# A four-layer graph network on one NeuronCore: LSTM operand copies on another engine, and a new order of work at the end of two layers

## The chip, the cores and the metric

The kernel runs on one core of a Trainium2 chip. The core has five engines with a queue of instructions each: TensorE (PE: matmuls and transposes; PEld is its loading of the stationary operand), VectorE (DVE), ScalarE (ACT), GpSimd (POOL) and SyncE (SP, which here only issues DMAs). They wait for one another through semaphores. The metric is the device time of one execution in microseconds (us), the median of several runs.

## The reference, cut to what matters

`x` is 128 batches x 64 nodes x 256 features in float32, `adj` a 64 x 64 matrix. Four layers of the form `x = x + gnn(relu(layernorm(x)), adj)` follow one another:

```
# layer 0: two graph convolutions, then an LSTM over windows of nodes
h = relu(adj @ (x @ Wg0 + bg0)); h = relu(adj @ (h @ Wg1 + bg1))
for p in 1, 2, 3, 4:                  # a window is p neighbouring nodes
    wins = h[:, :nw * p].reshape(B * nw, p, H)
    last = lstm_last(Wih[p-1], Whh[p-1], bih[p-1], bhh[p-1], wins)
    h[:, arange(nw) * p + (p - 1)] = last
# layer 1: attention over 512 edges, 4 heads
Xq, Xv = H @ W_lin.T, H @ W_val.T
e = sum(leaky_relu(Xq[:, src] + Xq[:, dst]) * a) + log(A0[src, dst] + EPS)
attn = softmax of e over the edges with the same src
Y = segment_sum(attn * Xv[:, dst], src) @ W_out.T
# layer 2: A_hat @ h, then two linear maps with batch norms
# layer 3: dense graph attention with a masked softmax
```

The layer norm is over the 256 features of a token. Each LSTM window of p nodes takes p steps of `g = x_t @ Wih.T + h @ Whh.T + bias` with the gates i, f, g, o.

## The kernel before, in words

The 8192 tokens are worked in 16 chunks of 512 tokens (128 tokens on the partitions, four such tiles to a chunk); a group is four chunks. The kernel is written with a framework that puts the instructions of each engine into a queue by its own scheduler; an instruction wrapped in `late` (L71 to L73) keeps its place in the program's order. Every queue runs in order. Tiles come from pools with a fixed number of buffers, and a load into a buffer waits until the last reader of its earlier content is done.

**Layer 0, convolutions** (`graph_convolutions`, L492, driven by the loop from L549). A chunk passes through stages; one round of the loop takes each chunk under way one stage on, oldest first, and the tables of a later layer are built in between. The class `Norm` (L78) takes mean and variance on VectorE, then 1/sqrt either on POOL with four small instructions (L99 to L102) or, with `root_on_scalar`, on ScalarE and VectorE (L95 to L97), and then ScalarE writes the scaled `h` (L109). Chunk 0 alone uses `root_on_scalar`. `bdA` is a block-diagonal matrix with `adj` twice; its matmul with `h` stands at L50.

**Layer 0, LSTM** (class `Step`, L582). The nodes' states lie transposed, features on partitions, in `hT`. The work is ordered by half of the groups, and in each half by phases w = 1, 2, 3, 4 (the window's length), in each phase by pairs of parts (so many windows at once) and by step t. A 2 x 2 block product is made with seven products in place of eight, so each operand is needed as seven blocks: three copies and four differences. `prepare` (L604) makes the seven for `x_t`: for w > 1 POOL copies (L619, L620) from the strided `hT` into the tile `xop`, VectorE subtracts (L621, L627, L628). It is called at the second-to-last gate of the step before. `product` (L638) runs the matmuls of one gate into PSUM tiles `pa`, `pb`, `pc`; ScalarE copies and functions (L666, L681, L686, L688) and VectorE adds (L682, L691, L696) empty them. The last step of a window ends with VectorE writing `hT` (L731). The class `Weights` (L414) loads a phase's weights with a DMA on SP and makes their four sums on POOL (L430): `wih` and `sih` with two buffers, `whh` and `shh` with one. `phase_over` asks for the next ones at the end of a phase. When a group has gone through w = 4, `group_out` (L763) transposes it back on PE (L165), adds it to the residual on VectorE (L168), stores it with a DMA of POOL's queue to `xa` in DRAM (L770) and loads the group of the second half into its place with SP (L773). It stands right behind the group's last gate.

**Layer 1** (L864 to L1216). `project`, `gather` and `score` run per tile and pair of tiles. Each group's `edge_softmax` (L968) is a generator whose steps are taken one by one between other work (`behind`, `step_behind`): scans and reciprocals on VectorE, transposes on PE (L997), VectorE's `attn` (L1000), eight indirect DMAs of POOL that scatter it into a dense field in DRAM (L1026), and two DMAs that bring the field back (L1012), one for each half of the partitions. Then, per chunk, `values_of` runs `weigh` (matmuls L1073 of the turned attention `att` with the values `xv`) and, one chunk later, `put_out` (matmuls L1093 with `wout`, VectorE's add of the residual L1103, the statistics of the next norm on VectorE L1109 and L1110, four small POOL instructions L1112 to L1115). `fetch` (L1041) loads `xv` and `xo` (four buffers) on SP and turns the attention with two copies (L1055, one on ScalarE and one on VectorE), one chunk ahead. `flush_stores` (L1149) stores the result to `xb`. Layer 2 begins with `scale_x` (L1197), loads of `xb` (L1230) and the matmuls with `bdH` (L50).

The order around the change:

```
for one in list(under_way):                      # convolutions, oldest first
...
if k == len(step.gates) - 2 and at + 1 < len(steps):
    steps[at + 1].prepare()
...
if step.w == MAX_SKIP and step.t == MAX_SKIP - 1:
    for c in range(2):
        group_out(step.g, c)
...
for n in range(4, NCH):                          # layer 1, second part
    for _ in range(6):
        step_behind()
```

## Time and profile before

| what | us |
|---|---|
| runs, device time | 2151.81, 2152.57, 2156.58 |
| median | 2152.57 |
| the profiled execution's own time | 2154.34 |
| its span | 2152.6 |
| PE busy | 2049.1 |
| DVE, ACT, POOL busy | 1354.9, 1123.4, 425.9 |
| layer 0, convolutions (0 to 80): PE busy | 65.4 |
| layer 0, LSTM (80 to 1310): PE busy | 1195.5 |
| layer 1 (1310 to 1765): PE busy | 425.8 |
| layer 2 (1765 to 1990): PE busy | 216.4 |
| layer 3 (1990 to 2152.6): PE busy | 146.0 |

The last five rows are from the trace's windows, with borders put by eye where one layer's matmuls give way to the next one's; the layers overlap a little. A stage's length less its PE time is the time in which PE stands. The mean granted clock of PE over the span was 0.981 of full speed. In the profile's lines an arrow in brackets, [1.56 <-DVE hT L731], gives the idle time ahead of an instruction and what ended it: engine, what it wrote, and its line in the kernel.

### The profile page before, as it was taken

What the parts mean: (1) busy time and instruction counts of PE and PEld (TensorE: products, weight loads), DVE (VectorE), ACT (ScalarE), POOL (GpSimd) and SP (SyncE); (2) the same over time, 40 slices, a digit from 0 to 9 for tenths busy, and PEclk for the clock granted to TensorE, in tenths of its full rate; (3) what the DMA queues carried; (4) which work ended last, traced back from release to release, by engine and by line L of the source; (5) the groups of instructions that cost most, each with busy time, mean ns of one, the idle gap of its engine ahead of it and who ended that gap; (6) DMA issues with size and microseconds to landing.
All of it is one profiled execution on the core that took longest, in us unless ns stands there. A gap on an engine that the chain in (4) does not pass through costs nothing.

```text
span 2152.6 us, 25600 instructions
## 1 busy us (share of the span) xinstructions
PE 2049.1 (95%) x9444; PEld 1362.6 (63%) x9444; DVE 1354.9 (63%) x2425; ACT 1123.4 (52%) x2160; POOL 425.9 (20%) x576
## 2 busy tenths in 40 slices
PE   7999999999899999999999998999999789999898
PEld 5777478766688746886668884333334665534686
DVE  6665666554555567556546555576776757786675
ACT  3344766544454467555445444566565356591444
POOL 4110011310301022003002112113212420000662
PEclk9999999999999999999999999999999999999899
DMA  8321000100100340001000024113314761022012
GB/s 282 103 85 68 0 21 1 40 0 1 39 1 1 118 156 20 0 1 40 0 24 16 0 69 152 59 40 103 93 60 126 207 208 59 0 69 88 30 60 69
DMA packets 94028, 135.06 MB, mean 63 GB/s; under 512 B 6352, under 2 KB 82000, under 8 KB 91600
## 3 DMA queue, kind: packets, MB, share of 16 engines
q1 hardware_dynamic: 87600, 109.11, 15.4%
q0 software_dynamic: 5696, 24.12, 3.8%
q8 instruction: 74, 1.21, 0.2%
q14 instruction: 50, 0.41, 0.1%
q10 hardware_dynamic: 608, 0.20, 0.0%
HBM read 87.28 MB, written 46.14 MB: 62 GB/s over the span
## 4 chain that ended last, share of the span: by engine, by line
PE 84%; DVE 5%; POOL 3%; ACT 3%; DMA 2%; issue 1%; ACTq 0%; POOLq 0%; DVEq 0%
PE pa L638 26%; PE bank L50 21%; PE pc L638 12%; PE pair L50 6%; PE pb L638 6%; PE pa L1279 5%; PE pc L1279 2%; PE pb L1279 1%; POOL sih L430 1%; PE bank L1093 1%; PE bank L165 1%; ACT gate L666 1%; POOL shh L430 1%; PE pair L1532 1%; PE pair L1564 1%
## 5 line engine op out<-in xcount | busy, mean ns | idle before, releaser
L666 ACT ACTIVATE gate<-gate,bias 128x256 f32<-128x256 f32 (+2 forms) x368 | 248.4, 678 | 227.5 <-DVE gate L682 118.9
L638 PE MATMUL pa<-xop,sih 128*128 128x256 f32 (+2 forms) x1056 | 352.0, 423 | 5.8 <-ACT gate L681 3.4
L638 PEld LDWEIGHTS pa<-xop,sih 128*128 128x128 f32 x1056 | 202.2, 193 | 79.8 <-issue 23.6
L638 PE MATMUL pc<-xop,wih 128*128 128x256 f32 (+2 forms) x736 | 252.5, 425 | 0.0
L619 POOL COPY xop<-hT 128x512 f32<-128x512 f32 (+1 forms) x44 | 60.3, 1371 | 799.2 <-issue 411.3
L638 PE MATMUL pa<-lstm_h,shh 128*128 128x256 f32 (+1 forms) x672 | 212.7, 398 | 0.0
L951 DVE SCALAR_TENSOR_TENSOR lr<-lr 128x1024 f32<-128x1024 f32 x128 | 153.5, 1230 | 87.1 <-ACT lr L950 84.3
L682 DVE TENSOR_TENSOR gate<-pb,gate 128x256 f32<-128x256 f32 (+2 forms) x184 | 87.4, 475 | 160.0 <-PE pb L638 123.5
L638 PEld LDWEIGHTS pc<-xop,wih 128*128 128x128 f32 x736 | 141.4, 192 | 52.3 <-issue 23.9
L696 DVE TENSOR_TENSOR gate<-pc,gate 128x256 f32<-128x256 f32 (+2 forms) x184 | 87.4, 475 | 106.9 <-PE pc L638 105.8
L638 PEld LDWEIGHTS pa<-lstm_h,shh 128*128 128x128 f32 x672 | 127.7, 190 | 30.2
L950 ACT COPY lr<-pair 128x1024 f32<-128x1024 f32 x128 | 125.0, 1015 | 34.3 <-PE pair L50 34.3
L638 PE MATMUL pc<-lstm_h,whh 128*128 128x256 f32 (+1 forms) x448 | 141.8, 398 | 0.0
L681 ACT COPY gate<-pa 128x256 f32<-128x256 f32 (+2 forms) x184 | 76.9, 418 | 124.2 <-PE pa L638 123.7
L666 ACT ACTIVATE gate<-pa,bias 128x256 f32<-128x256 f32 (+2 forms) x184 | 94.5, 514 | 83.7 <-PE pa L638 83.5
L50 PE MATMUL pair<-sd_hot,xq 64*128 64x512 f32 x512 | 134.4, 622 | 0.3 <-ACT lr L950 0.3
L50 PE MATMUL bank<-wlv,hT 128*128 128x512 f32 x256 | 122.7, 611 | 7.0 <-ACT hT L154 7.0
L638 PE MATMUL pb<-xop,wih 128*128 128x256 f32 (+1 forms) x320 | 103.3, 407 | 8.9 <-POOL xop L619 8.9
L691 DVE TENSOR_TENSOR gate<-pa,gate 128x256 f32<-128x256 f32 (+2 forms) x184 | 87.4, 475 | 37.2 <-PE pa L638 34.4
L638 PE MATMUL pa<-xop,wih 128*128 128x256 f32 (+1 forms) x320 | 102.7, 403 | 6.6 <-POOL xop L619 5.0
L638 PEld LDWEIGHTS pc<-lstm_h,whh 128*128 128x128 f32 x448 | 85.1, 190 | 20.1
L50 PEld LDWEIGHTS bank<-wlv,hT 128*128 128x128 f32 x256 | 44.8, 189 | 81.9 <-issue 62.1
(319 smaller groups left out, 3857.6 us busy)
## 6 DMA issues: line engine op xcount, KB each, us to landing
field<-sd_hot SPq DMA_DIRECT2D x8, 1152.0 KB, 10.8
wih<-in_WihT SPq DMA_DIRECT2D x8, 1024.0 KB, 5.1
xres<-in_x SPq DMA_DIRECT2D x16, 512.0 KB, 5.6
xa<-xres POOLq DMA_DIRECT2D x16, 512.0 KB, 5.9
xo<-xa SPq DMA_DIRECT2D x16, 512.0 KB, 4.3
dense<-field POOLq DMA_DIRECT2D x8, 1024.0 KB, 11.4
xb<-xo SPq DMA_DIRECT2D x16, 512.0 KB, 5.2
xin<-xb SPq DMA_DIRECT2D x16, 512.0 KB, 4.1
```

Source lines behind the costliest of these rows:

```text
L50: nc.tensor.matmul(o, lhsT, rhs, start=start, stop=stop)
L430: nc.gpsimd.tensor_tensor(o, x, y, op)
L619: nc.gpsimd.tensor_copy(self.as_nodes(v[:, 0:2]), self.nodes(slice(0, 2), t))
L638: ins = nc.tensor.matmul(p[:, : self.N], weights[kind, self.phase](k, q), x[k], start=first_ and kind == "ih", stop=kind == "hh" or not se ...
L666: nc.scalar.activation(out, in_, AF.Tanh if q == 2 else AF.Sigmoid, bias=bias[:, self.w - 1, 2 * q + j : 2 * q + j + 1],)
L681: nc.scalar.copy(blk[0, 0], pa[:, :N])
L682: nc.vector.tensor_tensor(blk[0, 0], pb[:, :N], blk[0, 0], ALU.add)
L691: nc.vector.tensor_tensor(blk[1, 1], pa[:, :N], blk[1, 1], ALU.add)
L696: nc.vector.tensor_tensor(blk[1, 0], pc[:, :N], blk[1, 0], ALU.add)
L950: nc.scalar.copy(lr, p)
L951: nc.vector.scalar_tensor_tensor(lr, lr, 0.2, lr, ALU.mult, ALU.max)
L1279: ins = nc.tensor.matmul(p, lhs[k], x[k], start=first_, stop=last_one, skip_group_check=True)
```

## The change

- `add_transposed`: the first transpose is `late`; so is the making of `mask3` (a table of layer 3) on VectorE. The copies into `bdA` go from VectorE to POOL.
- All 16 chunks' norms in the convolutions take `root_on_scalar`, and a round of the loop begins with the newest chunk.
- `prepare`: the two copies go from POOL to ScalarE.
- `phase_over`: the ih weights of a later phase are asked for eight gates later.
- `prepare` for the first w = 1 step of the second half is called at the last gate of the step before.
- `group_out` runs one gate (first half of the chunks) and two gates (second half) after the group's last gate, and after the last gate at the end of the layer.
- Layer 1: four steps of the last softmax follow the last `edges`, seven more come at chunk 4; the first of its transposes is `late`. Its field comes back in four DMAs instead of two.
- `fetch` loads `xv` and x two chunks ahead, and the copies of the attention are a function of their own, `turn_attention`, two chunks ahead also, with exceptions around chunk 12. The x of the last three chunks lies in tiles of other pools.
- The statistics and the POOL instructions behind `put_out` are a function `sums`; at chunks 3, 4 and 5 they are held back to a later chunk.

No arithmetic on the data changes but for the root (square root and reciprocal in place of a power).

```diff
                 k = (i2 * 2 + c) * P
-                nc.tensor.transpose(
+                ins = nc.tensor.transpose(
                     p[:, k : k + P], src[:, c, col + i2 * P : col + (i2 + 1) * P], ident
                 )
+                if k == 0:
+                    late(ins)
         nc.vector.tensor_tensor(
...
-            nc.vector.tensor_scalar(mask3, adj2, 0.0, NEG, ALU.is_equal, ALU.mult)
+            late(nc.vector.tensor_scalar(mask3, adj2, 0.0, NEG, ALU.is_equal, ALU.mult))
             yield
...
                 r = slice(h * T, (h + 1) * T)
-                nc.vector.tensor_copy(bdA[r, r], adjT2[r, :])
+                nc.gpsimd.tensor_copy(bdA[r, r], adjT2[r, :])
...
-                h = Norm(coming.pop(n), n == 0).all()
+                h = Norm(coming.pop(n), True).all()
                 if 4 <= n + 3 < NCH:
...
                     under_way.append(graph_convolutions(n))
-                for one in list(under_way):
...
+                for one in under_way[-1:] + under_way[:-1] if n < NCH else list(under_way):
                     if next(one, 0) == 0:
...
                 v = x[:, : 7 * N].rearrange("p (q n) -> p q n", n=N)
-                nc.gpsimd.tensor_copy(self.as_nodes(v[:, 0:2]), self.nodes(slice(0, 2), t))
-                nc.gpsimd.tensor_copy(self.as_nodes(v[:, 2:3]), self.nodes(slice(3, 4), t))
+                nc.scalar.copy(self.as_nodes(v[:, 0:2]), self.nodes(slice(0, 2), t))
+                nc.scalar.copy(self.as_nodes(v[:, 2:3]), self.nodes(slice(3, 4), t))
                 nc.vector.tensor_tensor(
...
             if ph + 2 < len(phases):
-                weights["ih", ph + 2] = Weights("ih", phases[ph + 2])
+                later_weights.append((slot + 8, ph + 2))
             nxt = ph + 1 if ph + 1 < len(phases) and phases[ph + 1] > 1 else ph + 2
...
+        later_weights = []
         tasks = [(s, q, k) for s in range(len(steps)) for k, q in enumerate(steps[s].gates)]
         flight = []
-        later = []
+        later, outs = [], []
         norm_steps = iter(())
...
                 at, k = new[0], new[2]
-                if k == len(step.gates) - 2 and at + 1 < len(steps):
+                while outs and outs[0][0] <= slot:
+                    group_out(*outs.pop(0)[1:])
...
+                new_half = at + 1 < len(steps) and at and steps[at + 1].w == 1 < step.w
+                if k == len(step.gates) - (1 if new_half else 2) and at + 1 < len(steps):
                     steps[at + 1].prepare()
...
             next(norm_steps, None)
+            while later_weights and later_weights[0][0] <= slot:
+                _, ph = later_weights.pop(0)
+                weights["ih", ph] = Weights("ih", phases[ph])
             if old:
...
                     if step.w == MAX_SKIP and step.t == MAX_SKIP - 1:
-                        for c in range(2):
-                            group_out(step.g, c)
+                        outs += [(slot + 1, step.g, 0), (slot + 2, step.g, 1)]
         for _ in norm_steps:
             pass
+        for _, g, c in outs:
+            group_out(g, c)
     psums["banks"] = None
...
             for ec in range(NE):
-                nc.tensor.transpose(p[:, ec * P : (ec + 1) * P], e[:, ec * P : (ec + 1) * P], ident)
+                ins = nc.tensor.transpose(p[:, ec * P : (ec + 1) * P], e[:, ec * P : (ec + 1) * P], ident)
+                if ec == 0 and g == NGR - 1:
+                    late(ins)
             yield
...
-            def bring_back(par):
+            def bring_back(par, parts=1):
+                for k in range(parts):
+                    part_back(par, k, parts)
...
+            def part_back(par, k, parts):
...
+                r, s = slice(par * T, (par + 1) * T), slice(k * 32 // parts, (k + 1) * 32 // parts)
                 back = nc.gpsimd.dma_start(
-                    out=dense[g][par * T : (par + 1) * T, :, :].rearrange("p s r -> p (s r)"),
-                    in_=fields1[2 * g + par][: T * T, :].rearrange("(t s) r -> t (s r)", t=T),
+                    out=dense[g][r, :, :].rearrange("p (o s) r -> p o s r", o=2)[:, :, s, :],
+                    in_=fields1[2 * g + par][: T * T, :].rearrange("(t o s) r -> t o s r", t=T, o=2)[
+                        :, :, s, :
+                    ],
                 )
...
                         yield
-            bring_back(0)
-            yield
-            bring_back(1)
+            if g == NGR - 1:
...
+                for k in range(2):
+                    for par in range(2):
+                        part_back(par, k, 2)
+            else:
+                bring_back(0)
+                yield
+                bring_back(1)
...
                 nc.sync.dma_start(out=xv, in_=xv_mem[n])
-            xt = xo.tile([P, 4, D], F32, tag="xo", name="xo")
+            if n < NCH - 3:
+                xt = xo.tile([P, 4, D], F32, tag="xo", name="xo")
+            else:
...
+                if n < NCH - 1:
+                    t = t1.tile([P, 2, CHUNK], F32, tag="hT1", name="xo_last")
+                else:
+                    t = w1.tile([P, 2, 2 * D], F32, tag="wlv", name="xo_last")
+                xt = t.rearrange("p c t -> p (c t)").rearrange("p (i d) -> p i d", d=D)
             nc.sync.dma_start(out=xt, in_=token_tiles(xa[n]))
+            fetched[n] = (xv, xt)
...
+        def turn_attention(n):
...
                 )
-            fetched[n] = (xv, xt, att)
+            turned[n] = att
...
-            xv, xt, att = fetched.pop(n)
+            (xv, xt), att = fetched.pop(n), turned.pop(n)
             yT = yp.tile([P, 8, 2, T], F32, tag="yT", name="yT")
...
             stores.append((n, xt))
+            unnormed.append((n, xt))
...
+        def sums(n, xt):
...
         NT = NTOK // P
-        dense, fetched, weighed, stores = {}, {}, [], []
...
-        def values_of(n):
...
-            if n not in fetched:
-                fetch(n)
+        dense, fetched, turned, weighed, stores, unnormed = {}, {}, {}, [], [], []
+        LAST = NCH - 4
...
+        def values_of(n, hold=False):
...
+            if n == 0:
+                for k in range(2):
+                    fetch(k)
+                    turn_attention(k)
             one = (n, *weigh(n))
-            if n + 1 < NCH:
-                fetch(n + 1)
+            if n + 2 < NCH:
+                fetch(n + 2)
+            if n == LAST:
+                turn_attention(n + 1)
+            if n + 2 < NCH and not LAST <= n + 2 < LAST + 2:
+                turn_attention(n + 2)
             flush_stores()
             flush_values()
...
+            if n + 1 == LAST:
+                turn_attention(LAST)
             weighed.append(one)
+            if not hold:
+                while unnormed:
+                    sums(*unnormed.pop(0))
...
             edges(q)
+            last_one = q == NT // 2 - 1
...
+            for _ in range(4 if last_one else 0):
+                step_behind()
...
             if q >= NT // 2 - 8 and q % 2:
-                values_of((q - NT // 2 + 8) // 2)
+                values_of((q - NT // 2 + 8) // 2, last_one)
...
         for n in range(4, NCH):
-            for _ in range(6):
-                step_behind()
+            if n == 4:
+                for _ in range(7):
+                    step_behind()
             if n == 6:
                 finish_behind()
-            values_of(n)
+            values_of(n, n in (4, 5))
             if n - 10 in first_x2:
...
         flush_stores()
+        while unnormed:
+            sums(*unnormed.pop(0))
     l01.close()
```

## The prediction

> **What bounds the kernel now.** I read the page's busy times and chain first, then the waits of PE, then the timeline at each PE gap, last the stages' windows with the granted clock.
>
> ```profile
> PE 2049.1 (95%) x9444; PEld 1362.6 (63%) x9444; DVE 1354.9 (63%) x2425; ACT 1123.4 (52%) x2160; POOL 425.9 (20%) x576
> ...
> PE 84%; DVE 5%; POOL 3%; ACT 3%; DMA 2%; issue 1%; ACTq 0%; POOLq 0%; DVEq 0%
> ```
>
> TensorE is the bound: 95% busy, 84% of the chain. The change alters no matmul, so it can only win the 2152.6 - 2049.1 = 103.5 us in which PE stands, and the time in which PE is busy at half clock. Whose waits those are:
>
> ```profile
> PE bank L165 <- DVE hT L731: 11.3, 4, 5.4
> PE bank L997 <- DVE e L993: 10.7, 1, 10.7
> PE bank L50 <- ACT h L109: 9.9, 3, 4.3
> PE pb L638 <- POOL xop L619: 8.9, 4, 2.6
> ...
> PE pair L1073 <- ACT att L1055: 5.3, 2, 4.7
> PE pa L638 <- POOL xop L619: 5.0, 2, 3.3
> ...
> PE bank L50 <- DVE xo L1103: 4.4, 1, 4.4
> ```
>
> Columns: us in total, number, longest. These seven lines hold 55.5 us, and each is a place that the diff edits. Not all of it goes: one L109 wait (4.28, at the start) and one L165 wait (5.42, the end of layer 0) keep their order. A gap costs twice, as windows around two gaps show:
>
> ```profile
> 432.40:435.80 3.40, 3.40 (x8) 2.04 (x7) 3.22 (x5) 0.44 (x1) 0.11 (x1) 0.50 0.00 0
> 436.00:448.00 12.00, 12.00 (x44) 8.08 (x43) 6.46 (x13) 7.82 (x14) 0.43 (x1) 1.00 0.00 0
> 575.80:582.60 6.80, 5.57 (x13) 4.50 (x14) 4.54 (x8) 2.00 (x5) 6.80 (x6) 0.50 0.00 0
> 1678.30:1688.50 10.20, 2.89 (x68) 2.52 (x68) 7.65 (x16) 0.00 (x0) 1.69 (x4) 0.50 0.32 104
> ```
>
> After the length: busy us of PE, PEld, DVE, ACT, POOL, then the granted clock. After the gap that ends at 431.98 PE is busy for 3.4 us at clock 0.50, and at 1.00 after that: half of the busy time, 1.7 us, is lost. In the second stretch it is 2.8, in the third 1.45. Such a stretch goes with ten of the gaps that the change addresses.
>
> The rule in the Trainium skill that bears on this ("TensorE: Matmul & The Clock Gate", "HAM oscillation") warns only of PE gaps longer than about 3.4 us. By it, gaps of 2.40, 2.64, 2.71 or 3.15 us would cost nothing in clock, and about 13 us of my sum would be missing (gain 41 instead of 54). The rows decide: the clock was 0.50 right after the gap of 2.40. I count the clock, but only where the trace shows it.
>
> **Part 1, convolutions of layer 0.** PE waits for `h` (L109) before 20.04 (2.51 us) and 32.13 (3.15 us): the newest chunk's scale stands on ScalarE behind older chunks' work, and its roots take four POOL instructions (ACT waited 9.50 us for POOL L102 there). The roots become one ScalarE square root (about 0.30 us where chunk 0 does it) and two VectorE instructions (0.18 and 0.16), issued first. Gain 2.51 + 3.15 + 1.7 (the half-clock stretch from 33.06) = 7.4 us. The cost, 15 x 0.30 on ScalarE and 15 x 0.34 on VectorE, lies beside PE's work: neither is busy more than seven tenths in any slice of this stage. Another activation-table load (1.28 us in the trace) comes in and is hidden in the same idle time. The deferred mask (VectorE) and the block-diagonal copies put on POOL are about 0.3 us of the start; I count zero, since the DMA of the adjacency ends last there.
>
> **Part 2, LSTM operands.** The timeline at one step's change and two others:
>
> ```profile
> 572.01 2.02 DVE L731 TENSOR_TENSOR hT<-gate 128x1344 f32<-128x1344 f32 x1 [1.52 <-ACT gate L666]
> 573.77 1.33 POOL L430 TENSOR_TENSOR sih<-wih 128x512 f32<-128x512 f32 x1 [25.19 <-PE pc L638]
> 575.05 1.93 POOL L619 COPY xop<-hT 128x512 f32<-128x512 f32 x1
> 577.03 1.22 PE L638 MATMUL pa<-xop,wih 128*128 128x256 f32 x2 [3.33 <-POOL xop L619]
> 577.59 1.47 DVE L627 TENSOR_TENSOR xop<-xop 128x256 f32<-128x256 f32 x1 [1.23 <-POOL xop L620]
> ...
> 844.97 0.70 PE L638 MATMUL pb<-xop,wih 128*128 128x256 f32 x2 [1.47 <-POOL xop L619]
> 845.31 0.42 DVE L627 TENSOR_TENSOR xop<-xop 128x256 f32<-128x256 f32 x1 [0.89 <-POOL xop L620]
> ...
> L619 POOL COPY xop<-hT 128x512 f32<-128x512 f32 (+1 forms) x44 | 60.3, 1371 | 799.2 <-issue 411.3
> ```
>
> POOL's in-order queue holds the copy behind a weight sum (L430), then takes 1.93 us for it. On ScalarE nothing of L430 stands before it. The 128x512 copy is not in the trace on ScalarE with this stride: bound 0.59 (unit stride, from the gates' 0.36 for 256 columns and 0.42 for 336) to 1.08 (L1055, strided). I take about 0.85, for the stride is nearer L1055's. A pair of copies is then 0.95 to 1.6 us, 1.2 to 2.1 in the third phase; all 44 put 45 to 77 us, say 57, on an engine that is about half busy here.
>
> PE's six stalls by xop are 2.40 (431.98), 3.33 (577.03), 2.64 (589.58), 1.47 (844.97), 2.40 (988.64), 1.63 (1131.99) = 13.9 us, and their half-clock stretches lose 1.7 + 2.8 + 1.6 + 0 + 1.7 + 1.7 = 9.5. Of these 23.4 some stay: at 577 VectorE ends hT only at 574.03 and a ScalarE copy ends near 575, where PE stood from 573.7, so 1.6 stay, and 1.9 at 1131.99, which is built alike. That leaves 20. Against it: in the 16 steps with t = 0 (half the matmuls per gate) the pair stands in front of gate functions whose PSUM banks PE wants back: 0 to 0.7 us each, 0.25 chosen, 4 in all. VectorE's 37.5 us of waiting for POOL's copies (L627) shrink; I count 1. Net 17.
>
> A second rule speaks here: the VectorE/GpSimd port pair is an exclusive lock ("SBUF — State Buffer", the diagram's reading). The rows show one side of it: L627 took 1.47 beside L430 and 0.42 alone. It would free VectorE of all slow subtractions if POOL fell silent; but the L430 sums stay, and at the phase changes, where the stall is, VectorE stays slow. By the rule alone 577 would go entirely (gain +1.6); I keep the 1.6 there.
>
> The later request of the ih weights (eight slots) I cost at nothing: their loads and sums wait for PE's release of the old tile in any case, and in the built order they stand in both queues (SP and POOL) still ahead of the hh weights at the two later phase changes. If it moved them past, POOL would be freer, not PE. The prepare of the second half's first w = 1 step goes one gate later: three VectorE subtractions with a gate's matmuls (3 us and more) as cover; without it, about 1.5 us once.
>
> **Part 3, transposes after a group's last gate.** PE waits for hT 1.56 (725.95), 2.71 (758.38) and 1.56 (1276.51), each with 0.35 more between its halves, and 1.7 of clock after the second: 8.6 us. One or two slots later hT is long done (L731 takes 2.0, a slot of PE work is 3 to 6). POOL's 4 stores and SP's 4 reloads per group go one or two slots later with it; the reload is needed groups later. Residue 1; gain 7.5.
>
> **Part 4, end of layer 1.** The last softmax stands on VectorE mixed with put_out's adds and statistics; PE waits 10.73 us for `e` at 1685.61. With its steps first, the chain that started at 1671.79 starts about 6.3 us earlier; `e` is ready near 1680.6 while PE, given one more chunk before it, comes at 1679.6: residue 1.1 of 10.73 + 1.45, gain 11.1. Behind the softmax on VectorE now wait the adds (L1103) that free PE's banks, and the sums; that can cost 0 to 3.4 us (the row of the four reciprocals, L991: 3.35). I take 0, for a chunk of matmuls (4.7 us, from 1692.20 to 1696.94) lies between. The eight indirect DMAs (about 1.3 us apart on POOL) then start near 1687 instead of 1695. The bring-back goes in two halves: two more DMAs in POOL's queue, smaller pieces, the first pair enough for chunks 12 and 13. I put its landing at 1710.5 (before, chunk 12's copy started at 1724.31), chunk 12 at 1711.7, PE at 1709.9: residue 2 of 4.66 + 1.7, gain 4.4. Layer 2's first matmul (1754.88) waited 4.45 for an add whose x arrived late, because xo has few buffers; three x's in other tiles end that, with 2.65 of clock. scale_x then waits for an h buffer, residue 1: gain 6.1. Together 21.6. The fetches go two chunks earlier on SP, ahead of stores that nobody waits for before layer 2.
>
> **Sum.** 7.4 + 17 + 7.5 + 21.6 = 53.5. The profiled execution took 2154.34 (span 2152.6); 1.8 above the runs' median 2152.57. So 2100.8 on its own scale, 2099 on the median's.
>
> **Rivals.**
> Stalls move to ScalarE (15%): its queue is in order, and a copy that waits for hT holds the gate functions behind it. ACT is the releaser of short PE waits already (L681, L686, L666: 6.6 us in all). If each of 44 pairs costs 0.5, it is 22 instead of 4: about 2117.
> The tail of layer 1 resists (12%): 14 chunks' traffic at DMA share 0.94 (window 1695 to 1715, 264 GB/s) may set the landing whatever the issue; then only the wait for `e` is won: 2099 + 10.5 = 2110.
> Everything goes (10%): no residue (8.6 in all), no ScalarE stall (4), and some of the untouched L165 wait: 2081 to 2087.
> Slower (3%): ScalarE becomes the LSTM's bound, every pair on the path. It decides from 53.5 / 44 = 1.2 us per pair beyond what is counted, or from 36.5 / 44 = 0.83 if the LSTM's gain of 17 is lost too; then, at the dearest pair of 1.65, 44 x 1.65 + 17 - 53.5 = 36 worse: 2189. ACT's 50% and DVE's slack speak against it.
> That it doesn't do what it says holds for the weights' delay only, costed at nothing.
>
> **How the numbers follow.** The main case has 60%: 2099, by itself 2089 to 2110. The range, 2083 to 2121, takes in most of the first three rivals. This kernel's runs differ by about 0.2% (4.3 us); beyond it: faster 0.96, same 0.02, slower 0.02.
>
> **What would show it.** In the profile after: no L619 row in PE's waits; L109 left with one wait; L165 at 5 to 6; the L997 wait below 2; PE busy near 2033 (some 16 of the half-clock time gone) and a span of 2099; ACT near 1185 busy, POOL near 320. The forecast is wrong if PE's waits for ACT gates grow by over 15 us, or if 0.50 stretches remain at 432 and 989.

## The result and the profile after

The changed kernel takes 2116.22 us (median of 4 runs, 2112.70 to 2117.12) against 2153.24 before (four runs, three of which stand in the table of the time before): ratio 0.9823, 95% interval 0.9806 to 0.984, 37 us faster. A later set of 5 runs gave 2117.40, ratio 0.9845 (0.9829 to 0.986). The forecast was 2099, its main case 2089 to 2110, its range 2083 to 2121. The profiled execution took 2112.7, the shortest of the four; its span is 2110.9, 41.7 less than the one before.

The page's busy times after, then PE's waits (us in total, times, longest):

```profile
PE 2028.9 (96%) x9444; PEld 1348.2 (64%) x9444; DVE 1352.1 (64%) x2453; ACT 1186.4 (56%) x2264; POOL 309.1 (15%) x432
```

```profile
PE pa L641 <- ACT gate L689: 10.1, 12, 1.5
...
PE pair L1112 <- ACT att L1094: 5.9, 2, 5.3
PE bank L165 <- DVE xres L170: 5.6, 8, 3.3
PE bank L165 <- DVE hT L734: 5.5, 1, 5.5
...
PE bank L50 <- ACT h L109: 3.9, 1, 3.9
...
PE pa L641 <- ACT xop L622: 3.1, 2, 1.5
...
PE pair L1112 <- DVE att L1094: 1.7, 1, 1.7
PE bank L1132 <- DVE xo L1142: 1.5, 1, 1.5
```

(L638 of before is L641 here, L619 is L622, L430 is L432, L686 is L689, L731 is L734, L168 is L170, L1055 is L1094, L1073 is L1112.) The waits for POOL's xop, for `e` and at bdH for xo are gone; L109 and hT keep one wait each, as foreseen. New or larger are four: the gate copy L689 on ScalarE, the adds L170 between transposes, the copies of the attention, and xop from ScalarE.

Where the time went is read best from lengths between landmarks on PE in the two traces (start of the instruction named, from the span's start):

| stretch | before | after | shorter by | forecast |
|---|---|---|---|---|
| to the first LSTM matmul | 199.8 | 192.6 | 7.2 | 7.4 |
| to the last group's transposes (1304.0; 1280.2) | 1104.2 | 1087.6 | 16.6 | 17 + 7.5 |
| to the first matmul with w2T of layer 2 (1883.6; 1845.0) | 579.6 | 564.8 | 14.8 | 21.6 |
| to the end (2152.6; 2110.9) | 269.0 | 265.9 | 3.1 | 0 |

The first row also corrects the table of the time before: the convolutions end at 199.8, not at the 80 that stands there as the border. The last row is mostly the clock: half-clock stretches at 1893.3 and 2142.5 have no counterpart in the second trace. The runs of the changed kernel differ by about as much.

The stretch of the LSTM in the two traces (length, then busy us of PE, PEld, DVE, ACT and POOL, granted clock, DMA share, GB/s):

```profile
199.79:1304.01 1104.22, 1069.76 (x4243) 801.08 (x4241) 646.68 (x1008) 595.39 (x1175) 169.56 (x152) 0.99 0.09 30
```

```profile
192.55:1280.17 1087.62, 1059.24 (x4242) 795.12 (x4241) 641.13 (x1008) 652.87 (x1263) 78.53 (x64) 1.00 0.08 29
```

Length less PE's busy time is the time in which PE stands: 34.5 us before, 28.4 after. So only 6.1 of the 16.6 us are less standing; 10.5 are shorter busy time for the same matmuls, the clock. The forecast's own terms for this stretch were 13.6 of standing (13.9 and 6.9 of waits and 1 of VectorE's, less 3.2 and 1 of residue and 4 for ScalarE) and 10.9 of clock: what is missing here is waits.

Two of the new waits, in the timeline after. First the step change at 577.03 of before and the gate that follows it (the arrow gives the idle time before):

```profile
563.73 1.11 ACT L622 COPY xop<-hT 128x512 f32<-128x512 f32 x1
564.75 0.64 ACT L623 COPY xop<-hT 128x256 f32<-128x256 f32 x1
564.89 0.70 PE L641 MATMUL pa<-xop,wih 128*128 128x256 f32 x2 [1.53 <-ACT xop L622]
...
565.99 1.17 DVE L630 TENSOR_TENSOR xop<-xop 128x256 f32<-128x256 f32 x1
566.84 1.45 POOL L432 TENSOR_TENSOR wih<-wih 128x512 f32<-128x512 f32 x1
...
572.06 1.06 ACT L721 ACTIVATE gate<-lstm_c 128x1024 f32<-128x1024 f32 x1 [0.65 <-DVE lstm_c L720]
573.03 1.10 ACT L669 ACTIVATE gate<-gate,bias 128x256 f32<-128x256 f32 x2
574.04 0.35 ACT L689 COPY gate<-pa 128x256 f32<-128x256 f32 x1
574.44 1.13 PE L641 MATMUL pa<-xop,sih 128*128 128x256 f32 x4 [1.38 <-ACT gate L689]
```

The 3.33 us of before at this step change (577.03) are 1.53 now, the predicted 1.6, and ScalarE's copies no longer stand behind L432. L630 still takes 1.17 us here with POOL's sums around it, as the forecast had it. At 574.44 PE waits for L689, which frees `pa`. No operand copy stands right ahead of that one on ScalarE: it had waited 0.65 us for VectorE's `lstm_c` and then ran three gate functions. The same place before:

```profile
585.29 1.06 ACT L718 ACTIVATE gate<-lstm_c 128x1024 f32<-128x1024 f32 x1
586.25 1.11 ACT L666 ACTIVATE gate<-gate,bias 128x256 f32<-128x256 f32 x2
587.26 0.35 ACT L686 COPY gate<-pa 128x256 f32<-128x256 f32 x1
...
589.58 1.22 PE L638 MATMUL pb<-xop,wih 128*128 128x256 f32 x2 [2.64 <-POOL xop L619]
```

There PE stood from 586.94; the same gate copy ended only at 587.61, and the rest of the wait was POOL's. So the gate copy was late there before, too, and the longer wait covered it. The six places at which PE waited for POOL's copies, found again by counting the LSTM's matmuls (to within two):

| before, at | us | after, at | us | released after by |
|---|---|---|---|---|
| 431.98 | 2.40 | 422.74 | 0.24 | L689 |
| 577.03 | 3.33 | 564.89 | 1.53 | L622 |
| 589.58 | 2.64 | 574.44 | 1.38 | L689 |
| 844.97 | 1.47 | 828.71 | 1.49 | L689 |
| 988.64 | 2.40 | 969.47 | 0.24 | L689 |
| 1131.99 | 1.63 | 1111.63 | 1.55 | L622 |

Of 13.9 us, 6.4 stay.

Then the transposes after a group's last gate:

```profile
722.19 1.23 DVE L613 TENSOR_TENSOR xop<-hT 128x1024 f32<-128x1024 f32 x1 [2.52 <-DMA hT<-hm]
722.50 1.04 PE L165 MATMUL bank<-ident,hT 128*128 128x128 f32 x8
...
726.13 1.28 DVE L170 TENSOR_TENSOR xres<-bank,xres 128x512 f32<-128x512 f32 x2
726.87 1.92 PE L165 MATMUL bank<-ident,hT 128*128 128x128 f32 x8 [3.33 <-DVE xres L170]
```

VectorE stood 2.52 us at L613, the first operand of the second half, for the reload of hT; the adds that free the transposes' banks stand behind it.

### The profile page after: what moved, and what is told of

It is laid out like the page before. It is cut to its first block, busy times and chain, and to the rows that moved or that the text cites. A ratio compares the mean times of both kernels' runs of the same rounds, so it can differ in the third digit from the quotient of the medians.

```text
span 2110.9 us, 25487 instructions
## 1 busy us (share of the span) xinstructions
PE 2028.9 (96%) x9444; PEld 1348.2 (64%) x9444; DVE 1352.1 (64%) x2453; ACT 1186.4 (56%) x2264; POOL 309.1 (15%) x432
## 4 chain that ended last, share of the span: by engine, by line
PE 81%; ACT 6%; DVE 6%; issue 4%; DMA 2%; POOL 1%; SPq 0%; ACTq 0%; POOLq 0%; DVEq 0%
PE pa L641 24%; PE bank L50 20%; PE pc L641 12%; PE pair L50 6%; PE pb L641 6%; PE pa L1341 5%; PE pc L1341 2%; ACT gate L669 2%; PE bank L1132 1%; PE pb L1341 1%; ACT gate L721 1%; PE pair L1626 1%; DMA xo<-xa 1%; PE pair L1594 1%; DVE lstm_c L720 1%
## 5 line engine op out<-in xcount | busy, mean ns | idle before, releaser
L641 PE MATMUL pa<-xop,sih 128*128 128x256 f32 (+2 forms) x1056 | 346.6, 417 | 11.8 <-ACT gate L689 10.1
L641 PEld LDWEIGHTS pa<-xop,sih 128*128 128x128 f32 x1056 | 198.5, 190 | 85.5 <-issue 20.9
L641 PE MATMUL pc<-xop,wih 128*128 128x256 f32 (+2 forms) x736 | 251.1, 423 | 0.0
L641 PE MATMUL pa<-lstm_h,shh 128*128 128x256 f32 (+1 forms) x672 | 212.7, 398 | 0.0
L641 PEld LDWEIGHTS pc<-xop,wih 128*128 128x128 f32 x736 | 139.8, 190 | 51.2 <-issue 22.5
L641 PEld LDWEIGHTS pa<-lstm_h,shh 128*128 128x128 f32 x672 | 127.7, 190 | 30.2
L641 PE MATMUL pc<-lstm_h,whh 128*128 128x256 f32 (+1 forms) x448 | 141.8, 398 | 0.0
L641 PE MATMUL pa<-xop,wih 128*128 128x256 f32 (+1 forms) x320 | 101.8, 400 | 5.4 <-ACT xop L622 3.1
L432 POOL TENSOR_TENSOR sih<-wih 128x512 f32<-128x512 f32 x8 | 10.8, 1350 | 632.2 <-DMA wih<-in_WihT 440.7
L641 PE MATMUL pb<-xop,wih 128*128 128x256 f32 (+1 forms) x320 | 100.5, 398 | 0.0
L641 PEld LDWEIGHTS pc<-lstm_h,whh 128*128 128x128 f32 x448 | 85.1, 190 | 20.1
```

Of the source, the lines that this page charges most:

```text
L641: ins = nc.tensor.matmul(p[:, : self.N], weights[kind, self.phase](k, q), x[k], start=first_ and kind == "ih", stop=kind == "hh" or not se ...
```

## The experiments

All ratios are to the kernel before, run beside them, with 95% intervals. The stretch of the trace between the landmarks of the table is given where it is the sharper measure: seven traces whose LSTM is that of the changed kernel lie between 1086.7 and 1089.7 there, mean 1087.8. On the chip of the first four runs the kernel before itself took 2160.34, so their ratios are compared with each other and with stretches, not finely with the other sets. The unaltered changed kernel was run again as reference:

> The changed kernel itself, unaltered, as the reference on this chip for the other runs of the set. Expected from its first measurement: 0.982 of the kernel before.

Measured 2117.40, ratio 0.9845 (0.9829 to 0.986): the interval overlaps that of the first measurement.

**Operand copies back on POOL**

```
-                nc.scalar.copy(self.as_nodes(v[:, 0:2]), ...)
-                nc.scalar.copy(self.as_nodes(v[:, 2:3]), ...)
+                nc.gpsimd.tensor_copy(self.as_nodes(v[:, 0:2]), ...)
+                nc.gpsimd.tensor_copy(self.as_nodes(v[:, 2:3]), ...)
```

> The changed kernel with the two operand copies of prepare back on POOL, nothing else. Theory (ScalarE's in-order queue gave back part of the gain): PE's waits for POOL xop return with about 14 us and 5 to 6 half-clock stretches (up to 9.5 us), PE's waits for ACT gates fall from 13.6 (10.1 of it L689) to about 6.6, and the 3.1 of ACT xop go: 2116 + 14 + 9.5 - 7 - 3 = about 2129. Rival (the copies' move is worth the full 17 of the forecast, the loss is elsewhere): 2133 and the L689 wait unchanged. Rival (it is worth nothing): 2116.

Measured 2129.61, ratio 0.9860 (0.9842 to 0.9878). PE's waits in its trace:

```profile
PE pb L641 <- POOL xop L622: 9.3, 4, 2.7
...
PE pa L641 <- POOL xop L622: 5.0, 2, 3.3
...
PE pa L641 <- ACT gate L689: 1.6, 6, 0.6
```

14.3 us of POOL waits are back and L689 falls from 10.1 to 1.6. The LSTM stretch is 1099.5, so the move is worth 11.7 of the forecast's 17; by the runs it is 11.9 against the kernel with the attention in two tiles (2117.71, same chip), whose LSTM is that of the changed one. The trace before would make it more: after the gaps of 2.40 at 424.58 and 1.65 at 1122.05 the clock stays at 1.00 in this trace, and at the same places before it was 0.50, 3.4 us of the forecast's clock. That L689's wait comes with the move is shown. Why it comes is shown in part: at four of its twelve places (271, 340, 818, 887; 3.4 us) an operand copy stands among the last four ScalarE instructions ahead of it; two (574, 829; 2.9 us) stand where PE waited for POOL before, and at the first of them the gate copy was late before, too. For the other six no reason is shown.

**Copies on ScalarE twice**

```
                 nc.scalar.copy(self.as_nodes(v[:, 0:2]), ...)
+                nc.scalar.copy(self.as_nodes(v[:, 0:2]), ...)
                 nc.scalar.copy(self.as_nodes(v[:, 2:3]), ...)
+                nc.scalar.copy(self.as_nodes(v[:, 2:3]), ...)
```

> The changed kernel with each of the operand copies on ScalarE issued twice (the second writes the same values again). Theory: in the 16 steps with t = 0 the second pair (about 1.3 us) adds to PE's waits for gates and for xop nearly in full, 10 to 20 us, and in the 28 others it is hidden: 0.5 to 1% slower than the changed kernel. Rival ScalarE has slack throughout: no difference. Rival ScalarE is the bound in the whole LSTM: 44 x 1.3 = 57 us, 2.7% slower.

Measured 2130.19, ratio 0.9903 (0.9888 to 0.9918), 12.8 us above the changed kernel of the same set. The stretch is 1099.8, 12.0 more. The second copies keep ScalarE busy for 68.3 us more, so 18% of it reaches PE: ScalarE neither has slack throughout nor is it the bound. PE's wait for the gate copy grows only from 10.1 to 12.8, that for `xop` itself from 3.1 to 12.0.

**Copies of w = 2 on POOL, the others on ScalarE**

```
+                copy = nc.scalar.copy if self.w > 2 else nc.gpsimd.tensor_copy
```

> The changed kernel with the operand copies of the phases w = 2 back on POOL, those of w = 3 and 4 on ScalarE. Theory (ScalarE's queue holds up the gate copy L689 that PE waits for, and POOL was late only at a few phase changes): of PE's waits for ACT gates the w = 2 part, 7.6 us in the two halves, goes; POOL's 1.5 to 1.8 at the start of each w = 2 phase comes back: 4 to 6 us faster than the changed kernel, 0.2 to 0.3%. Rival (the L689 waits have another cause, such as VectorE being released earlier): they stay, no difference.

Measured 2115.27, ratio 0.9828 (0.9815 to 0.9842); the intervals of this and of the reference overlap. In the trace the gate copy's waits in w = 2 fall to 0.8 in all, POOL is waited for 1.45 at 280 and 1.46 at 826 (before only in the second half, 1.47), and the stretch is 1086.3: 1.5 shorter than the mean, not 4 to 6, and the seven traces spread over 3.0. PE stands 25.1 us in it, 3.3 less than in the changed kernel, so one reason stands in the trace: the gap of 1.54 at 1108.67 brought a half-clock stretch here and in the reference did not (below).

**Both halves of group_out one gate later**

```
-                        outs += [(slot + 1, step.g, 0), (slot + 2, step.g, 1)]
+                        outs += [(slot + 1, step.g, 0), (slot + 1, step.g, 1)]
```

> The changed kernel with both halves of group_out one gate after the group's last gate (the second was two gates after). Theory: the gap of 3.33 us before the transposes at 726.87 is VectorE's queue: the operand step of the second half (L613) stands there ahead of the adds and waits 2.52 us for the reload of hT that the first half of group_out has only just asked for. With both halves together the adds stand ahead of it; the gap and its half-clock stretch go: 3 to 5 us faster, about 2112. Rival (the gap is PSUM banks or the stores): it stays, 2116. Against the theory: the block of 32 transposes may bring back gaps of 0.35 between the adds.

Measured 2111.92, ratio 0.9779 (0.9762 to 0.9796). The stretch is 1082.7, 5.1 shorter. In its timeline:

```profile
714.47 1.25 PE L165 MATMUL bank<-ident,hT 128*128 128x128 f32 x8 [0.35 <-DVE xres L170]
715.91 1.26 PE L165 MATMUL bank<-ident,hT 128*128 128x128 f32 x8 [0.18 <-DVE xres L170]
717.35 1.26 PE L165 MATMUL bank<-ident,hT 128*128 128x128 f32 x8 [0.18 <-DVE xres L170]
721.52 1.23 DVE L613 TENSOR_TENSOR xop<-hT 128x1024 f32<-128x1024 f32 x1 [2.19 <-DMA hT<-hm]
```

VectorE still waits for the reload, 2.19 us, but nothing that PE needs stands behind it: gap and half-clock stretch are gone. The order in VectorE's queue was the cause.

**group_out right behind the last gate, as before**

```
-                        outs += [(slot + 1, step.g, 0), (slot + 2, step.g, 1)]
+                        for c in range(2):
+                            group_out(step.g, c)
```

> The changed kernel with group_out right behind the group's last gate, as before. Theory (the delay was worth 8.6 us less the new gap of 3.3 with its half-clock stretch and what the transposes still wait between): 3 to 5 us slower than the changed kernel. The forecast's own number for the part: 7.5 us slower.

Measured 2118.33, ratio 0.9841 (0.9825 to 0.9857), not told apart from the reference by time. Its stretch is 1090.1: the delay as made was worth 2.3 us, hardly more than the traces' spread, and in the form of the experiment before 7.4 (1090.1 - 1082.7), the forecast's 7.5.

**Oldest chunk first in the convolutions**

```
-                for one in under_way[-1:] + under_way[:-1] if n < NCH else list(under_way):
+                for one in list(under_way):
```

> The changed kernel with the convolutions' rounds begun at the oldest chunk again, roots still on ScalarE. It parts the 7.2 us that the stretch up to the first LSTM matmul became shorter. Theory (the order decides: the newest chunk's four scalings stood behind older chunks' ScalarE work): the gaps of 2.5 and 3.2 us come back for the larger part, 4 to 7 us slower than the changed kernel. Rival (the roots on POOL, with 1.1 us for the power and four steps, were the delay): 0 to 2 us slower.

Measured 2122.45, ratio 0.9855 (0.9837 to 0.9874). The first LSTM matmul starts at 197.05: of the 7.2 us, 4.4 go with the order and 2.8 with the roots and the other edits of this stage (the late mask, the copies on POOL), which were not tried alone. The clock is in both: PE stands 14.6 us in this stage before, 11.1 here and 9.7 in the changed kernel, and there are one, two and no half-clock stretches of 1.7. By standing alone the larger part goes with the roots and these other edits. A gap of 1.99 at 21.24 is back and none at 32.

**Layer 1 from the softmax on as before**

```
-            for _ in range(4 if last_one else 0):
-                step_behind()
...
+            for _ in range(6):
+                step_behind()
...
-            if n + 2 < NCH:
-                fetch(n + 2)
+            if n + 1 < NCH:
+                fetch(n + 1)
...
```

> The changed kernel with layer 1 from the softmax on as it was before (order, fetches, bring-back); layer 0 as changed. Theory (part 4 is worth what the two profiles differ by between the last transposes of layer 0 and layer 2's dense part, 14.8 us): 2131, PE again waiting 10.7 for e at L997's place, 4.7 for att and 4.4 for xo. Forecast's own number for the part, 21.6: 2138.

Measured 2134.18, ratio 0.9879 (0.9859 to 0.9899). The wait for `e` is back as it was (10.7), and at bdH it is 5.6. The third stretch is 587.2, longer even than before (579.6): PE stands 4.2 us longer there, 3.3 of it short waits at the matmuls with the attention that the profile puts down to "issue" and that all four traces of this chip show. So the part was worth 14.8 us by the two profiles and up to 22 by this one, which is the slowest of its four runs; by the medians it is 16.5 (2134.18 against 2117.71 of the kernel with the attention in two tiles).

**Attention in two tiles**

```
-            dense[g] = attp.tile([P, T, T], F32, tag="dense", name="dense")
+            dense[g] = [attp.tile([P, 2, 16, T], F32, tag="dense", name="dense", bufs=6) for _ in range(2)]
...
-  dense[g][:, :, o * 32 + m * 8 : o * 32 + m * 8 + 8]
+  dense[g][m // 2][:, o, m % 2 * 8 : m % 2 * 8 + 8, :]
```

> The changed kernel with each group's dense attention in two tiles (first and second half of each o), so that a copy for chunk 12 depends on the two DMAs of its own half; every group's field comes back in four DMAs. Theory: in the changed kernel chunk 12's copy waits for all four parts, so the split brought nothing; now it starts when the second DMA lands (8 us after its issue at 1675.9, near 1684.5 instead of 1690), PE's waits for att (5.3 + 1.7 + half of a 6.8 us half-clock stretch) shrink by 7 to 10 us: about 2107 to 2109. Rival (the four transfers share the bandwidth with the x loads and the stores, and land together): about 2115, and the copy at 1689 as before.

This kernel changes the computation: the tile is cut along its second axis, while a chunk needs all of that axis and its own columns of the third; so its copies read other elements, and its time tells only of the waits. That is at the same time the finding: in the changed kernel, too, the DMAs are cut along the axis that every chunk needs in full. The split can let no chunk start early. Measured 2117.71, ratio 0.9806 (0.9789 to 0.9823). The copy for chunk 12 depends on two parts only and starts at 1692.9, 13.3 us after the last of the four issues; in the changed kernel 12.9. But it does not start then because a transfer landed:

```profile
1691.99 1.01 ACT L1123 COPY yT<-pair 128x1024 f32<-128x1024 f32 x1 [1.76 <-PE pair L1114]
1692.90 1.08 ACT L1096 COPY att<-dense 128x512 f32<-128x512 f32 x1
```

It follows the copy of the chunk ahead without idle time (in the changed kernel ScalarE stood 8.52 us before it, for the DMA), for on this chip PE came later to that chunk. So the trace does not show when the parts landed, and neither theory nor rival is decided by it. The third stretch is 566.8, no shorter.

**Stores held back**

```
         def flush_stores(n=NCH):
+            held = [one for one in stores if 9 <= one[0] <= 11 and n < 13]
```

> The changed kernel with the stores of chunks 9, 10 and 11 of layer 1 (0.5 MB each) held back until chunk 13, after the transfers that bring back the last group's attention. Theory (those transfers are set by the bandwidth that they share): 1.5 of the some 5 MB under way are out of the way, the copy for chunk 12 starts 3 to 4 us earlier after the last of the four issues than the 13 to 14 us seen so far, and PE's wait before chunk 12 or the short waits in the chunk ahead shrink: 2 to 5 us faster than the changed kernel. Rival (a transfer of 64 partitions in pieces of 4 KB has its own limit): still 13 us, no difference.

Measured 2115.52, ratio 0.9831 (0.9818 to 0.9844). The copy came 13.6 us after the last issue, PE waited 6.1 and 1.6 for it: the theory fell, these stores are not what the transfer waits for. Its rival, a limit of the transfer's own, is taken up in the next run.

**Two DMAs of 1 MB for the last group**

```
-                for k in range(2):
-                    for par in range(2):
-                        part_back(par, k, 2)
+                bring_back(0)
+                bring_back(1)
```

> The changed kernel with the last group's attention brought back by two DMAs of 1 MB, as the other groups' are, in place of four of 0.5 MB. Each chunk's copy reads all four parts. Theory (the split only moves 0.5 MB of the first half of the partitions behind the wait for the last indirect DMA, and the parts share one limit): the copy for chunk 12 comes 2 to 3 us earlier, about 12 us after the last indirect DMA has landed as in the kernel before (12.0 there, 14.6 in the changed kernel): 1 to 4 us faster than the changed kernel, ratio to the kernel before 0.982 to 0.984 on a chip where the changed one has 0.984. Rival (smaller parts go faster or the order is of no matter): no difference or slower.

Measured 2117.06, ratio 0.9837 (0.9821 to 0.9852): no difference. But the wait has changed its name:

```profile
PE pair L1110 <- DMA xv_in<-xv: 4.9, 1, 4.9
...
PE pair L1110 <- DVE att L1092: 1.2, 1, 1.2
...
PE pair L1110 <- ACT att L1092: 0.6, 1, 0.6
```

Now the values of chunk 11, fetched two chunks ahead, are late. The edit did not do that: the unaltered changed kernel, run again, waits for them too (3.3 us). Nor is the attention earlier: its copy starts at 1689.35, 13.3 us after the second issue; PE meets it later. The same trace shows what sets those 13.3 us. For the first group the same two DMAs of 1 MB are issued at 1438.44 and 1440.73, and the second takes 11.9 us. The two windows (columns as above):

```profile
1438.00:1452.60 14.60, 14.26 (x62) 4.89 (x60) 9.80 (x16) 8.70 (x16) 5.34 (x9) 1.00 0.77 182
1672.00:1689.30 17.30, 12.43 (x164) 10.36 (x163) 7.52 (x25) 5.57 (x8) 12.92 (x28) 0.82 0.98 249
```

In the first of them, 2.65 MB move, all from POOL's queue, in the second 4.34. So most of the time is the transfer's own, as the rival of the run before had it, and the traffic around it adds about 1.4 us. What limits the transfer stays open.

**Three edits together**

> Three edits on the changed kernel together: both halves of group_out one gate after the group's last gate, the operand copies of w = 2 on POOL, the last group's attention back in two DMAs. Theory (they act at different places and add): 4 to 8 us from the first, 2 to 4 from the second, 1 to 4 from the third: 8 to 14 us faster than the changed kernel, 0.4 to 0.6%. Rival: the third is swallowed by a later transfer (x or values of chunk 11 to 13): 6 to 8.

Measured 2112.39, ratio 0.9814 (0.9798 to 0.9829). The LSTM stretch is 1081.8, only 0.9 less than with group_out alone, so the second edit shows no gain beyond the spread. At the tail PE waits longer for the values than in any other trace:

```profile
1667.71 0.50 SPq L1074 DMA_DIRECT2D xv_in<-xv  x1
...
1682.97 1.34 PE L1111 MATMUL pair<-att,xv_in 64*64 64x64 f32 x40 [8.22 <-DMA xv_in<-xv]
```

The load took 15.1 us from issue to landing; an earlier load of `xv_in` in the same trace (issued at 1646.8) 4.6. In the windows of that trace (length, then busy us of PE, PEld, DVE, ACT and POOL, granted clock, DMA share, GB/s):

```profile
1640.00:1656.00 16.00, 16.00 (x269) 13.09 (x271) 15.96 (x37) 7.64 (x8) 3.00 (x7) 1.00 0.51 166
1656.00:1671.00 15.00, 15.00 (x298) 12.67 (x288) 13.69 (x43) 6.01 (x6) 9.27 (x11) 1.00 0.92 303
1671.00:1686.00 15.00, 6.78 (x91) 5.72 (x84) 4.92 (x17) 3.92 (x7) 13.03 (x29) 0.76 1.02 237
```

While PE stands, all DMA engines are busy (share 1.02), as they are in the changed kernel between 1675 and 1690 (1.04, 260 GB/s). So the rival of the last expectation holds. This kernel is no faster than the one with group_out alone (2111.92); the two come from different sets and are not told apart.

## Why the prediction was right or wrong

The measured 2116.22 lies outside the main case (2089 to 2110) and inside the range only because that takes in the rivals. Of the 53.5 us forecast, the runs gave 37. Missing are 5.3 in part 2, 5.2 in part 3 and 6.8 in part 4. Measured part by part (7.2, 11.7, 2.3 and 14.8) the sum is 36.0; in the LSTM the parts give 14.0 of 16.6, and the 2.6 left over are less than the 3.4 of clock that the trace with the copies on POOL lacks by chance.

**Part 1** was right: 7.4 forecast, 7.2 measured, and the two gaps are gone.

**Part 2**: 17 forecast, 11.7 measured. The step that failed is the residue: "That leaves 20" keeps a wait at 577 and at 1131.99 only. Those two were right (1.53 and 1.55; from "near 575" and 573.7 the sum would have been 1.3, not 1.6). But PE stands at 589.58's and 844.97's places too, 1.38 and 1.49, for the gate copy: POOL's wait was taken off in full, and what ended next at the same matmul was not looked for. The other term, "0 to 0.7 us each, 0.25 chosen, 4 in all", came out near: PE's waits for ACT gates rose from 6.6 to 13.6, and away from the six places from 6.6 to 10.2. The rest of the difference is the clock, 9.5 counted, of which the trace with the copies on POOL lacks two stretches (3.4). The cost of the copies was low as well: a pair was put at 0.95 to 1.6 us, 57 in all; it is 1.1 for w = 2 but 1.8 for w = 3 and 4, and 68.3 in all. In ScalarE's group rows after (the first two mix w = 2 and w = 4):

```profile
L622 ACT COPY xop<-hT 128x512 f32<-128x512 f32 x32 | 28.9, 904 | 1.6 <-DVE hT L734 1.6
L623 ACT COPY xop<-hT 128x256 f32<-128x256 f32 x32 | 17.7, 552 | 0.0
L622 ACT COPY xop<-hT 128x672 f32<-128x672 f32 x12 | 13.7, 1138 | 0.7 <-DVE hT L734 0.6
L623 ACT COPY xop<-hT 128x336 f32<-128x336 f32 x12 | 8.0, 669 | 0.0
```

The first rival named the waits for ACT gates; they grew by 7.0, not by 22. That its number, 2117, is the measured time is luck: parts 3 and 4 fell short as well.

**Part 3**: 7.5 forecast, 2.3 measured. The step that failed is "the reload is needed groups later". The group of the second half takes the first group's place, and its first operand is prepared one gate later, in VectorE's queue ahead of the second half's adds. With that order mended, the part gave 7.4.

**Part 4**: 21.6 forecast, 14.8 measured. The softmax step was right, even cautious: `e` is no longer waited for. The bdH step was right: 4.4 became 1.2, with no half-clock stretch. The step that failed is "the first pair enough for chunks 12 and 13": every chunk needs all four parts, and PE waited 5.3 and 1.7 for the copies and 1.5 for an add behind a late x, where a residue of 2 was kept. After that PE ran at half clock from 1689.5 to 1696.3, counted at nothing. The landing, put at 23.5 us after the start of the indirect DMAs (1687 to 1710.5), came 28.4 us after it (1661.55; the copy starts at 1689.98). The second rival's mechanism is shown in half: the DMA engines are full for 15 us, and which late transfer PE meets (attention, x or values) differs from trace to trace; but the attention's own transfer takes nearly as long without the other traffic (11.9 against 13.3). In all kernels with the new layer 1 the third stretch lay between 564.3 and 567.7. On the chip of the first four runs the short waits put down to "issue" (4.4 to 4.7 us in total at those matmuls with the new layer 1) stand in place of the wait for the attention; their cause stays open.

**Not tried alone** were the weights' delay, costed at nothing, the later `prepare` of the second half, the statistics held back and the fetches ahead.

**The clock** was counted rightly where gaps went: the stretches at 33, 432, 576, 589, 989 and 1132 are gone from the trace after, as are those at 1678 and 1753; those at 760 and 1726 came again behind the new waits (at 727 and 1690). PE's busy time fell by 20.2 us for the same matmuls (16 forecast), but 3.4 of it are the stretches at 1893.3 and 2142.5, behind which nothing was changed: luck of that trace. In the second trace of the changed kernel it fell by 16.2. By the rule that was weighed (the Trainium skill, "TensorE: Matmul & The Clock Gate", "HAM oscillation": no gaps above about 3.4 us), the first six would have cost nothing, for their gaps were 1.63 to 3.33; in the trace before they cost 11.2 us.

The signs named ahead came as said (L109, L997, PE, ACT and POOL busy), but for L165: 11.1 us in two rows (5.5 and 5.6) where 5 to 6 were foreseen.

## What to carry to other kernels

Work moved to an idle-looking engine is paid for where that engine frees something for the bound: look for the in-order copy that empties a PSUM bank before you count its idle share. Before you take a wait off in full, look what ends next at the same matmul. When a step is put later, list what it starts (here a reload) and what else its engine's queue will then meet first. When a transfer is cut so that a consumer can start early, check that the cut lies along the axis that the consumer splits; measure the same transfer where little else moves, before you blame the traffic; and once the DMA engines are full, taking one transfer's wait away uncovers the next one's.

## What the runs showed that was not expected

A gap of the same length does not always bring the same clock. After 1.54 and 1.53 us without a matmul at the same step of the LSTM, the clock was 0.50 in one trace (w = 2 copies on POOL) and 1.00 in the other (the changed kernel again); the two windows:

```profile
1108.80:1112.00 3.20, 3.20 (x8) 2.55 (x9) 3.08 (x6) 1.87 (x4) 3.12 (x3) 0.50 0.10 33
```

```profile
1112.00:1115.20 3.20, 3.20 (x15) 2.84 (x16) 3.06 (x6) 2.48 (x6) 2.05 (x2) 1.00 0.16 53
```

The trace has 8 matmul records of PE in the one and 15 in the other. It holds for longer gaps too: after 2.40 us at 431.98 the kernel before had 0.50, and after 2.40 us at the same matmul the kernel with the copies on POOL had 1.00. A sum that counts 1.7 us for every short gap, or nothing for it, is off by that much per gap, and edits worth 2 to 4 us drown in it.
